# A graph layer on one Trainium2 core: the row that VectorE compares places with, in PSUM instead of SBUF

## The chip, the core and the metric

The kernel runs on one core of a Trainium2 chip. The metric is device time in microseconds: the median of the runs. PE is TensorE (matrix products), DVE is VectorE, ACT is ScalarE, POOL is GpSimd, SP is SyncE, which here only issues transfers. SBUF is the core's working memory with 128 partitions; PSUM is where products land, eight banks of 128 partitions by 512 fp32 numbers.

## The reference

One layer of a graph network with a gated update, over 12,500 nodes with 128 features and 400,000 edges with 32 features; the edges are sorted by their destination `dst`.

```python
h = jnp.maximum(_layernorm(x), 0.0)
e = jnp.concatenate([h[src], h[dst], edge_attr_32], axis=-1)
m = jax.nn.relu(e @ w1 + b1) @ w2 + b2
agg = jax.ops.segment_sum(m, dst, num_segments=12500)
gi, gh = agg @ w_ih + b_ih, h @ w_hh + b_hh
r, z = sigmoid(gi_r + gh_r), sigmoid(gi_z + gh_z)
n = tanh(gi_n + r * gh_n)
out = x + (1 - z) * n + z * h
```

## The kernel before, in words

**First stage (lines 207 to 334).** The nodes are normalised in chunks of four times 128. PE transposes each chunk into a PSUM tile named `oh` (line 296), DVE or ACT copies it to `hT_all` (line 315), a second product with the first 128 rows of `w1` lands in `pre` (line 325), and is copied and stored to DRAM as the table `A` (lines 305 and 320): `A` holds each node's contribution as a source. The tile `oh` comes from the pool `ps2`, which hands out two banks in turn.

**Edges (lines 842 to 935).** The edges are worked through in 391 pairs of up to 8 tiles of 128 edges; a pair is two units `u = 2k` and `2k + 1`. For each tile of most pairs, POOL issues a gather (line 145): an indirect transfer that reads 128 rows of `A` (for the first ten pairs, of `x`) by the indices in `src_i`, which lie in SBUF, into `G`. For 43 pairs nothing is gathered; there ACT (line 789, 19 pairs) or DVE (line 796, 24 pairs) copies the columns of `hT_all` one by one, at addresses loaded to registers, and PE multiplies them (line 612). Both are spread over the units from a list (`jobs`), not placed by a planner.

Since the edges are sorted, the destinations of a pair lie in two windows of 32 consecutive nodes. For each pair, DVE copies the windows' columns to `hw` (line 519), PE multiplies them with the second part of `w1` into an `oh` tile (line 526, the *product*), and DVE adds the bias on the way to `RW` (line 535). DVE builds a one-hot matrix of places as the left side of the next product (line 500), PE makes `pre` from it (line 601), DVE adds the gathered rows (line 626, the *add*), and ACT applies the relu (line 632).

To sum by destination, DVE builds a second one-hot matrix, `OH` (line 553, the *compare*): for each edge, the place of its destination in its window (`dloc`, fp16, in SBUF, one number for each partition and tile) is compared with the row 0..31 (`iota`, fp16, in SBUF, filled by POOL at line 117). Both operands are read with repeats, for 256 results in a partition, fp32. PE multiplies `OH` with the relu's output (line 645), and DVE and ACT take the sums out (lines 653 and 654).

**Nodes (lines 657 to 736).** After every 14 pairs the sums of a block of 512 nodes are placed, and the gates are computed in single steps (lines 699 to 734, among them DVE's lines 712, 715, 724, 726, 728 and 734), spread over the following units.

**Order.** The order on each engine is the one in which the program is written (`manual_schedule`); waits are put in where tiles depend on each other. In a pair, DVE makes the compare for pair k + 3 in the second unit, then the add, the bias step (535), and the window copy for pair k + 4 (519); PE makes the product for pair k + 3 in the first unit. POOL's queue holds little but the gathers in order; a gather waits only until its `G` buffer (7 in a ring, 4 more at the start) is free. One more user of an `oh` tile is `check_windows` (line 460), once, near the end. A branch for other inputs (line 1036 on) isn't taken here.

Of the kernel before, what the change touches and what calls it, by code (L numbers as in the profile page):

```python
# [8 lines left out]
F32 = mybir.dt.float32  # L9
# [10 lines left out]
N, E, D, DE = 12500, 400000, 128, 32  # L20
# [5 lines left out]
NP = T // PAIR + 1  # L26
NU = 2 * NP

V = 32
# [26 lines left out]
def tile_gnn(ctx: ExitStack, tc: tile.TileContext, x, src, srcT, dstT, dstP, eaT, eaP, w1, b1, w2T, b2,  # L56
             wih, bih, whh, bhh, out):
    nc = tc.nc
# [8 lines left out]
    ge = early.enter_context(tc.tile_pool(name="ge", bufs=EARLY, side="right"))  # L67
    ps2 = ctx.enter_context(tc.tile_pool(name="ps2", bufs=2, space=bass.MemoryType.PSUM))
    ps1 = ctx.enter_context(tc.tile_pool(name="ps1", bufs=1, space=bass.MemoryType.PSUM))
    dram = ctx.enter_context(tc.tile_pool(name="dram", bufs=1, space=bass.MemoryType.DRAM))  # L70

    def tiles(k):
        return (0 if k == 0 else SUP0 + (k - 1) * PAIR, SUP0 + k * PAIR)
# [11 lines left out]
    for m, n in SPREAD.items():  # L85
        lo, hi = {"dve": (JOBS0 + 3, NP - 9), "act": (JOBS0 + 11, NP - 6)}[m]
        for i in range(n):
            k = lo + int((i + 1) * (hi - lo) / n)
# [27 lines left out]
    iota = const.tile([128, V], F16, name="iota")  # L116
# [86 lines left out]
    def relu_norm(o, xi, st):  # L203
        nc.scalar.activation(o, xi, AF.Relu, bias=st[:, 1:2], scale=st[:, 0:1])
# [4 lines left out]
    with tc.tile_pool(name="pp", bufs=3) as pp:  # L209
# [6 lines left out]
        def nodes(t, i0, n, P):  # L216
            return t[i0 * 128:i0 * 128 + n * P, :].rearrange("(p i) f -> p i f", p=P)


        def columns(b, c, e):  # L220
            i0, n = bats[b]
            t = hT_all[:, i0 * 128:i0 * 128 + n * PB(b)].rearrange("f (p i) -> f i p", i=n)
            return t[:, c:e, :]

        def load(b):
            if b < len(bats):
                i0, n = bats[b]
                P = PB(b)
                xs[b] = pp.tile([128, 8, D], F32, name="xs", bufs=5)
                nc.sync.dma_start(xs[b][:P, :n, :], nodes(x, i0, n, P))  # L230
# [3 lines left out]
        def stat(b):  # L234
            if b < len(bats):
                i0, n = bats[b]
                mvs[b] = bn(pp, lambda j: xs[b][:PB(b), j, :], PB(b), n)

        def sqr(b):
            if b < len(bats):  # L240
                mvs[b] = bn_sqrt(pp, mvs[b], PB(b), bats[b][1])

        def fin(b):
            if b < len(bats):
                i0, n = bats[b]
                bn_fin(pp, st_all[:, i0:i0 + n, :], mvs.pop(b), PB(b), n)
# [32 lines left out]
        def chunk(q):  # L279
            b, c = chunks[q]  # L280
            i0, n = bats[b]
            return b, i0, c, min(n, c + 4), PB(b), (i0 + c) * 128

        pts, pas = {}, {}
        NC = len(chunks)
        for q in range(NC + 3):
            if q < NC:
                b, i0, c, e, P, n0 = chunk(q)
                if c == 0:
                    stat(b + 2)  # L290
                    fin(b + 1)
            if 1 <= q <= NC:
                b, i0, c, e, P, n0 = chunk(q - 1)
                pts[q - 1] = ps2.tile([128, 512], F32, name="oh")
                for j in range(c, e):
                    nc.tensor.transpose(pts[q - 1][:, (j - c) * P:(j - c + 1) * P],
                                        xs[b][:P, j, :], ident[:P, :P])
                if e == bats[b][1]:
                    load(b + 5)
            if q >= 3:  # L300
                b, i0, c, e, P, n0 = chunk(q - 3)
                if c == 0:
                    asb[b] = pp.tile([128, 8, D], F32, name="asb", bufs=2)
                copy = nc.scalar.copy if q % 4 == 2 else nc.vector.tensor_copy
                copy(asb[b][:P, c:e, :], pas.pop(q - 3)[:P, :e - c, :])
            if q < NC:
                b, i0, c, e, P, n0 = chunk(q)
                for j in range(c, e):
                    relu_norm(xs[b][:P, j, :], xs[b][:P, j, :], st_all[:P, i0 + j, :])
                if e == bats[b][1]:  # L310
                    sqr(b + 2)
            if 1 <= q <= NC:
                b, i0, c, e, P, n0 = chunk(q - 1)
                copy = nc.scalar.copy if q % 4 == 0 else nc.vector.tensor_copy
                copy(columns(b, c, e), pts.pop(q - 1)[:, :(e - c) * P].rearrange(
                    "f (i p) -> f i p", i=e - c))
            if q >= 3:
                b, i0, c, e, P, n0 = chunk(q - 3)
                if e == bats[b][1]:
                    nc.sync.dma_start(nodes(A, i0, e, P), asb[b][:P, :e, :])  # L320
            if 2 <= q <= NC + 1:
                b, i0, c, e, P, n0 = chunk(q - 2)
                pas[q - 2] = ps2.tile([128, GRP, D], F32, name="pre")
                for j in range(c, e):
                    nc.tensor.matmul(pas[q - 2][:P, j - c, :], columns(b, j, j + 1)[:, 0, :],
                                     w1a, start=True, stop=True)
        for b0, b1, n in ((0, 1, BAT[0]), (1, 12, 8), (12, 13, BAT[12])):
            i0 = sum(BAT[:b0])
            for b in range(b0, b1):
                i = i0 + (b - b0) * n  # L330
# [2 lines left out]
                    st_all[:, i:i + n, :].rearrange("p i o -> p (i o)"))  # L333
        nc.sync.dma_start(stats[NFULL * 128:N, :], st_all[:N - NFULL * 128, NFULL, :])

    p3 = ctx.enter_context(tc.tile_pool(name="p3", bufs=3, reuse_waits="tile"))
    TOT = p3.tile([128, 2 * BW - DMIN], F32, name="TOT", bufs=1)
    DEG = p3.tile([33, 2 * BW - DMIN], F32, name="DEG", bufs=1)
# [15 lines left out]
    pm = ps1.tile([128, 512], F32, name="misc")  # L354
# [65 lines left out]
    pm = ps1.tile([128, 512], F32, name="nd")  # L420
# [29 lines left out]
    def check_windows():  # L450
        m = const.tile([128, 2], F32, name="lim1")
        nc.vector.tensor_reduce(m[:, 0:1], lim[:, 0, :], AX.X, ALU.max)
        nc.vector.tensor_reduce(m[:, 1:2], lim[:, 1, :], AX.X, ALU.min)
        bad = const.tile([128, 2], F32, name="bad")
        nc.vector.tensor_scalar(bad[:, 0:1], m[:, 0:1], float(V - 1), None, op0=ALU.is_gt)
        nc.vector.tensor_scalar(bad[:, 1:2], m[:, 1:2], 0.0, None, op0=ALU.is_lt)
        one = const.tile([128, 1], F32, name="one")
        nc.vector.tensor_tensor(one, bad[:, 0:1], bad[:, 1:2], op=ALU.max)
        pm = ps2.tile([128, 512], F32, name="oh")
        nc.tensor.transpose(pm[0:1, :128], one, ident)  # L460
        f = const.tile([1, 8], F32, name="flags")
        nc.vector.tensor_reduce(f[:, 0:1], pm[0:1, :128], AX.X, ALU.max)
        nc.vector.tensor_reduce(f[:, 6:7], off_f, AX.XY, ALU.max)
        nc.vector.tensor_reduce(f[:, 7:8], off_f, AX.XY, ALU.min)
        nc.vector.tensor_scalar(f[:, 1:2], f[:, 6:7], float(BW - V - SHIFT), None, op0=ALU.is_gt)
        nc.vector.tensor_scalar(f[:, 5:6], f[:, 7:8], 0.0, None, op0=ALU.is_lt)
        nc.vector.tensor_reduce(f[:, 2:3], step_f, AX.X, ALU.max)
        nc.vector.tensor_scalar(f[:, 3:4], blk_f[:, NB - 1:NB], float(N - BW), None,
                                op0=ALU.not_equal)
        nc.vector.tensor_copy(f[:, 4:5], f[:, 5:6])  # L470
        nc.vector.tensor_reduce(f[:, 6:7], f[:, 0:6], AX.X, ALU.max)
        nc.vector.tensor_copy(flag, f[:, 6:7])
# [31 lines left out]
    bases, PB_, HW = {}, {}, {}  # L504
# [17 lines left out]
    def window_product(k):  # L522
        if k >= NP:
            return
        PB_[k] = ps2.tile([128, 512], F32, name="oh")
        nc.tensor.matmul(PB_[k][:2 * V, :D], HW.pop(k).rearrange("p a v -> p (a v)"), w1b,  # L526
                         start=True, stop=True)

# [8 lines left out]
    def onehot(k):  # L537
        if k >= NP:
            return
        t0, t1 = tiles(k)  # L540
        OH[k] = OHB[k % len(OHB)]
        for a in range(2) if k == 0 else (None,):
            if a is None:
                o, s = OH[k].rearrange("p j a v -> p a j v"), slice(t0, t1)
                d = dloc[:, s].rearrange("p (a j) -> p a j", a=2)[:, :, :, None]
                shape = [128, 2, GRP, V]
                i = iota[:, None, None, :]
            else:
                e = min(t1, (a + 1) * GRP)
                o, d = OH[k][:, :e - a * GRP, a, :], dloc[:, a * GRP:e, None]  # L550
                shape = [128, e - a * GRP, V]
                i = iota[:, None, :]
            nc.vector.tensor_tensor(o, d.to_broadcast(shape), i.to_broadcast(shape),  # L553
                                    op=ALU.is_equal)

# [294 lines left out]
    for k in range(3):  # L850
        window_copy(k)
        window_product(k)
        window_rows(k)
# [35 lines left out]
    for u in range(NU):  # L889
        k, h = divmod(u, 2)  # L890
# [145 lines left out]
    f = nc.values_load(flag[0:1, 0:1], min_val=0, max_val=1)  # L1036
# [67 lines left out]
```

## Time and profile before

| | |
|---|---|
| runs before | 3594.44, 3597.59, 3604.85 us; median 3597.59 |
| profiled execution | 3598.83 us, its span 3597.1 us |
| busy, share of the span | PE 74%, DVE 68%, ACT 70%, POOL 75% |
| mean granted clock of TensorE | 0.778 |
| DMA, mean over the span | 89 GB/s |

How to read the profile: a span is the time from the first to the last instruction of one profiled execution. A line of the table of groups gives source line, engine, operation, output and inputs with their shapes and the count, then the busy time in us with the mean of one in ns, then the idle time of the engine just before them and what ended it. "Issue" is time in which the engine waited for nothing that the profile shows: its own issuing, or loads of registers, which are not counted as busy. In the waits, a line says who waited for whom, for how many us in total, how often, and the longest. In the timeline, a line starts with start and duration in us.

### The profile page before, as it was taken

How to read it: one execution, taken by the hardware profiler on the slowest of the kernel's cores; microseconds unless marked ns; L12 is line 12 of the kernel's file. 1: busy time of each engine (PE TensorE's matmuls, PEld its weight loads, DVE VectorE, ACT ScalarE, POOL GpSimd, SP SyncE). 2: the span in 40 equal slices, each digit the busy share in tenths (PEclk: the TensorE clock that was granted, in tenths of full speed). 3: DMA queues.
4: the chain of work that ended last, by engine and by line, in shares of the span. 5: the costliest groups of instructions: out<-in, count | busy, mean ns of one | idle time of the engine just before them, and what ended most of it. 6: DMA issues, size and time to landing. Idle time of an engine off the chain costs nothing. (4 is left out here: it accounts for less than half of the span.)

```text
span 3597.1 us, 76803 instructions
## 1 busy us (share of the span) xinstructions
PE 2664.4 (74%) x13674; PEld 1618.5 (45%) x13674; DVE 2445.7 (68%) x16547; ACT 2506.7 (70%) x20936; POOL 2694.2 (75%) x2789
## 2 busy tenths in 40 slices
PE   7697677677767776876777777677767776776876
PEld 6454344444434443443444444444444443443443
DVE  8766667677667667667666677676667677766652
ACT  5445567777777777777777777777777677767771
POOL 7677777777777777777777777777777777777774
PEclk9787888787877877777786888787777778786777
DMA  6333333333333333333333333333333333333331
GB/s 207 86 100 87 86 88 88 92 86 89 87 88 85 87 89 85 89 86 89 86 86 89 86 88 88 92 87 88 88 87 86 85 89 84 89 85 87 81 86 41
DMA packets 145458, 321.60 MB, mean 89 GB/s; under 512 B 58913, under 2 KB 64844, under 8 KB 144967
## 3 DMA queue, kind: packets, MB, share of 16 engines
q0 software_dynamic: 88992, 182.43, 20.7%
q1 hardware_dynamic: 55831, 134.16, 13.5%
q14 instruction: 379, 3.10, 0.3%
q8 instruction: 112, 1.84, 0.2%
q10 hardware_dynamic: 144, 0.07, 0.0%
HBM read 302.60 MB, written 13.84 MB: 88 GB/s over the span
## 5 line engine op out<-in xcount | busy, mean ns | idle before, releaser
L145 POOL DMA_INDIRECT G<-A,src_i x2704 | 2620.3, 969 | 835.3 <-issue 780.1
L789 ACT COPY HE_act<-hT_all 128x4 uint8 x19456 | 1983.0, 189 | 585.6 <-issue 583.7
L796 DVE SCALAR_TENSOR_TENSOR both<-hT_all 128x4 uint16 x12288 | 1097.0, 155 | 954.0 <-issue 947.2
L601 PE MATMUL pre<-RW,L 128*128 128x256 f32 x3128 | 1171.0, 503 | 730.5 <-DVE G L626 633.8
L601 PEld LDWEIGHTS pre<-RW,L 128*128 128x128 f32 x3128 | 677.1, 241 | 1068.8 <-DVE G L626 811.0
L632 ACT ACTIVATE RB<-G 128x512 f32<-128x512 f32 x676 | 424.5, 628 | 353.5 <-issue 143.4
L645 PE MATMUL seg<-RB,OH 128*32 128x129 f32 x6250 | 642.8, 340 | 4.3 <-ACT dcol L654 4.3
L626 DVE TENSOR_TENSOR G<-pre,G 128x512 f32<-128x512 f32 x676 | 462.5, 684 | 64.1 <-DMA G<-A,src_i 41.7
L645 PEld LDWEIGHTS seg<-RB,OH 128*32 128x32 f32 x6250 | 349.5, 130 | 232.2 <-issue 127.9
L526 PE MATMUL oh<-w1b,hw 128*64 128x128 f32 x782 | 213.0, 364 | 123.8 <-DVE hw L519 120.4
L535 DVE TENSOR_TENSOR RW<-oh,b1b 32x128 f32<-32x128 f32 x782 | 217.2, 278 | 11.5 <-PE oh L526 6.2
L526 PEld LDWEIGHTS oh<-w1b,hw 128*64 128x64 f32 x782 | 91.6, 166 | 294.2 <-DVE hw L519 210.6
L500 DVE TENSOR_SCALAR L<-Ld,node_of 64x512 f32<-64x512 int32 x391 | 192.2, 492 | 0.7 <-issue 0.6
L553 DVE TENSOR_TENSOR OH<-dloc,iota 128x256 f32<-128x256 f16 (+1 forms) x392 | 161.0, 411 | 0.2
L676 PE MATMUL nd<-spot,sums 64*128 64x40 f32 x782 | 116.9, 319 | 0.0
L676 PEld LDWEIGHTS nd<-spot,sums 64*128 64x128 f32 x782 | 113.0, 229 | 7.9 <-issue 7.9
L653 DVE COPY sums<-seg 64x128 f32<-64x128 f32 x391 | 107.1, 274 | 4.9 <-PE seg L645 3.7
L640 PE MATMUL seg<-zrow 1*64 1x129 bf16 x391 | 106.4, 272 | 3.0 <-ACT dcol L654 3.0
L519 DVE COPY hw<-hT_all 128x64 f32 x391 | 87.6, 224 | 24.6 <-issue 23.4
L801 DVE COPY HE_dve<-both 128x512 uint8<-128x512 uint8 x192 | 88.0, 458 | 6.6
L145 POOL DMA_INDIRECT G<-in_x,src_i x77 | 73.0, 948 | 25.1 <-issue 22.9
L640 PEld LDWEIGHTS <-zrow 1*64 1x64 bf16 x391 | 43.4, 111 | 94.7 <-issue 94.7
(148 smaller groups left out, 1605.0 us busy)
## 6 DMA issues: line engine op xcount, KB each, us to landing
Ld<-in_dstP SPq DMA_DIRECT2D x390, 128.0 KB
L<-in_eaP SPq DMA_DIRECT2D x195, 256.0 KB
G<-A,src_i POOLq DMA_INDIRECT x2704
xb<-in_x SPq DMA_DIRECT2D x28, 256.0 KB
out<-xb SPq DMA_DIRECT2D x28, 256.0 KB
xs<-in_x SPq DMA_DIRECT2D x11, 512.0 KB
A<-asb SPq DMA_DIRECT2D x11, 512.0 KB
src_i<-in_srcT SPq DMA_DIRECT2D x19, 80.0 KB
```

Source lines behind the costliest of these rows:

```text
L145: nc.gpsimd.indirect_dma_start(out=G[k][:, j, a, :], out_offset=None, in_=table, in_offset=bass.IndirectOffsetOnAxis(ap=src_i[c][:, i:i + ...
L500: nc.vector.tensor_scalar(Ls[k // QP][:2 * V, c], Ds[k // QP][:, c], node_of[:, k:k + 1], None, op0=ALU.is_equal)
L526: nc.tensor.matmul(PB_[k][:2 * V, :D], HW.pop(k).rearrange("p a v -> p (a v)"), w1b, start=True, stop=True)
L535: nc.vector.tensor_tensor(RW[k % 4][s, a, :], pm[s, :D], b1b[s, :], op=ALU.add)
L553: nc.vector.tensor_tensor(o, d.to_broadcast(shape), i.to_broadcast(shape), op=ALU.is_equal)
L601: nc.tensor.matmul(PP[u][:, 2 * i:2 * i + 2, :], Ls[k // QP][:, c0:c0 + 128], RW[k % 4], start=True, stop=not raw)
L626: nc.vector.tensor_tensor(RT[u], PP.pop(u), RT[u], op=ALU.add)
L632: nc.scalar.activation(o[:, :, :D], RT.pop(u), AF.Relu)
L645: nc.tensor.matmul(SEG[k][V * a:V * (a + 1), :D + 1], OH[k][:, j, a, :], RB[u % 3][:, (j % 2) * 2 + a, :D + 1], start=False, stop=all(b != ...
L676: nc.tensor.matmul(pt[:, bass.ds(offs[i], V + SHIFT)], sums[:, i, :], spot, start=False, stop=i == n - 1)
L789: nc.scalar.copy(he[:, e * 4:e * 4 + 4], column(v))
L796: nc.vector.scalar_tensor_tensor(both[:, (e0 % PIECE + i) // 2, :], column(vals[i + 1]), 256.0, column(vals[i]), op0=ALU.mult, op1=ALU.add)
```

## The change

Two PSUM tiles `wide` of 128 x 512 are allocated once and for all, in place of the two rotating `oh` tiles of pool `ps2`; the number of banks in use stays the same. The first stage's transposes, the products and `check_windows` use them in turn. After the first stage, DVE copies `iota` (fp16) into columns 128 to 159 of both (fp32 there). A product writes columns 0 to 127 of the bank `k % 2`; the compare for pair k reads the row from the other bank, `(k + 1) % 2`. The compare's first operand `dloc` and its output stay in SBUF.

```diff
+    wide = [ps1.tile([128, 512], F32, name=f"wide{i}") for i in range(2)]
...
-                pts[q - 1] = ps2.tile([128, 512], F32, name="oh")
+                pts[q - 1] = wide[q % 2]
...
+    for w in wide:
+        nc.vector.tensor_copy(w[:, D:D + V], iota)
     p3 = ctx.enter_context(tc.tile_pool(name="p3", bufs=3, reuse_waits="tile"))
...
-        pm = ps2.tile([128, 512], F32, name="oh")
+        pm = wide[(NP - 20) % 2]
         nc.tensor.transpose(pm[0:1, :128], one, ident)
...
-        PB_[k] = ps2.tile([128, 512], F32, name="oh")
+        PB_[k] = wide[k % 2]
         nc.tensor.matmul(PB_[k][:2 * V, :D], HW.pop(k).rearrange("p a v -> p (a v)"), w1b,
...
         OH[k] = OHB[k % len(OHB)]
+        row = wide[(k + 1) % 2][:, D:D + V]
...
-                i = iota[:, None, None, :]
+                i = row[:, None, None, :]
...
-                i = iota[:, None, :]
+                i = row[:, None, :]
             nc.vector.tensor_tensor(o, d.to_broadcast(shape), i.to_broadcast(shape),
                                     op=ALU.is_equal)
```

## The prediction

> **What bounds the kernel now.** I read four views in this order: the table of costliest groups, the waits, the chain that ended last, and the timeline. The groups:
>
> ```profile
> L145 POOL DMA_INDIRECT G<-A,src_i x2704 | 2620.3, 969 | 835.3 <-issue 780.1
> L626 DVE TENSOR_TENSOR G<-pre,G 128x512 f32<-128x512 f32 x676 | 462.5, 684 | 64.1 <-DMA G<-A,src_i 41.7
> L553 DVE TENSOR_TENSOR OH<-dloc,iota 128x256 f32<-128x256 f16 (+1 forms) x392 | 161.0, 411 | 0.2
> L145 POOL DMA_INDIRECT G<-in_x,src_i x77 | 73.0, 948 | 25.1 <-issue 22.9
> ```
>
> POOL issues 2704 + 77 = 2781 gathers. Their busy time is 2620.3 + 73.0 = 2693.3 us and the gaps ahead of them 835.3 + 25.1 = 860.4 us: 3553.7 us together, and the last gather ends at 3553.9 of a span of 3597.1. So POOL does nothing but gathers, back to back. The waits say why the gaps are there:
>
> ```profile
> POOL G L145 <- issue: 803.0, 2635, 0.3
> POOL G L145 <- PE misc L586: 11.6, 1, 11.6
> DVE G L626 <- DMA G<-A,src_i: 41.7, 20, 4.3
> DVE node_of L365 <- POOL place_c L360: 13.1, 1, 13.1
> ```
>
> Each line gives microseconds, times and the longest. The gap is a fixed 0.3 us of issue; POOL waits for a buffer only once (11.6 us, in the start). The others wait for POOL: the add of line 626 sat 41.7 us until gathers landed. The chain that ended last shows the same at its start: gather, issue, gather, then a tail of 43 us without gathers.
>
> ```profile
> 3551.59 0.30 issue
> 3551.90 0.95 POOL G L145
> 3552.84 0.30 issue
> 3553.15 0.77 POOL G L145
> ```
>
> So every nanosecond that a gather gets shorter moves the end, as long as the consumers keep up. The commonest gather lasts 0.944 us (the median of the view of line 145; its minimum is 0.940, its maximum 2.132). 2693.3 - 2781 x 0.944 = 68.0 us are excess. The timeline shows where excess comes from (start, duration):
>
> ```profile
> 1110.20 0.42 DVE L553 TENSOR_TENSOR OH<-dloc,iota 128x256 f32<-128x256 f16 x1
> 1110.20 1.23 POOL L145 DMA_INDIRECT G<-A,src_i  x1 [0.30 <-issue]
> ```
>
> ```profile
> 420.33 0.69 DVE L626 TENSOR_TENSOR G<-pre,G 128x512 f32<-128x512 f32 x1
> 420.75 0.94 POOL L145 DMA_INDIRECT G<-A,src_i  x1 [0.30 <-issue]
> ```
>
> ```profile
> 1198.65 0.41 DVE L553 TENSOR_TENSOR OH<-dloc,iota 128x256 f32<-128x256 f16 x1
> 1198.66 1.22 POOL L145 DMA_INDIRECT G<-A,src_i  x1 [0.30 <-issue]
> ```
>
> A gather that starts with a compare of line 553 takes 1.22 to 1.23 us; one that starts inside the add of line 626, with 0.27 us of it left, takes 0.94. The compare has both inputs in SBUF, the add has one in PSUM. Over the whole trace, gather by gather: the excess is (end of the compare) - (start of the gather) - 0.124 us, with a spread of 0.004. So 0.124 us after its start a gather needs something that the compare holds to its end. 117 gathers fit this for line 553 within 25 ns, with **26.1 us** of excess. Against it: 153 gathers reach that point in the middle of an add of line 626 and have a mean excess of -0.1 ns and a largest of 3 ns. Lines 712, 715 and 734, with the SBUF input first and the other in PSUM as in the changed compare, give 21 more, none over 3 ns. The steps at 724, 726 and 728, same shape but both inputs in SBUF, do stall gathers (29 of them, 10.5 us).
>
> The 26.1 follows from rows too: a gather starts every 3553.7 / 2781 = 1.278 us, a compare holds 0.412 us, so by chance 391 x 0.412 x 0.412 / (2 x 1.278) = 26.0 us.
>
> **The change part by part.**
>
> *The compare's second input moves to PSUM (391 pairs).* By the rows above the compare then has its operands where lines 712, 715 and 734 have theirs, and stalls no gather: -26.1 us. Not all is won: 31 of the 117 gathers began over 0.06 us ahead of the compare, and most of those were held first by the step before it, nearly always line 796, which also has two SBUF inputs and hands over to the compare. Held to that step's end alone they would keep 3.6 us. Net **-22.5 us** on POOL. The other blockers stay (line 500 11.6 us, line 801 5.9, line 796 3.8, the gate steps).
>
> [...]
>
> *The compare's own duration.* At 512 elements the rows with one PSUM input last 668 to 687 ns (lines 626, 712, 715, 734) and those with two SBUF inputs 672 to 683 (724, 726, 728); at 128 elements 278 (line 535) against 283 (line 553, first pair). So -15 to +15 ns on 411: -6 to +6 us of DVE over 391 compares. A farther row is the plain copy of 128 elements: 274 ns from PSUM (line 653), 203 from SBUF (line 436), 71 ns more. I take 0, by the rows of the same operation, and keep 71 ns for the range. DVE isn't the last to end: the 41.7 us at line 626 is its cover. In the trace the time from a pair's gather to its add shrinks from 36 us at 500 to 23 at 2000; first at 2400 does the add wait for the gather (1.7 us behind). So the consumers are a little faster than POOL and have about 41.7 us in hand; the gain uses 22.5 and leaves 19.2. 33.0 of the 41.7 lie after 3200, mostly in the last pairs, where the hand-made columns are over and only POOL is late.
>
> [...]
>
> *Two copies of the row to PSUM*, 128x32. Nearest rows: 181 ns (line 553 at 32 elements) and 274 (line 653). About 0.4 us on DVE, ahead of the 13.1 us in which line 365 waits for POOL: nothing. Uncovered it is 0.4 us.
>
> *Fixed banks for the rotating pair* (lines 296, 460, 526). In the built order, the steady part has the same instructions with the same waits on every engine; the product still waits for hw and alternates over two banks, and the bank that a compare reads gets its next product only after the window copy that DVE makes behind that compare. In the first stage some matmuls lose a wait on PE, and one ScalarE copy gains one on DVE; behind it stand the later ScalarE copies and the loads of `xs`. POOL issues raw gathers until 98.6 us without waiting for that stage, and DVE idles 13.1 us before line 365: a shift of some us is hidden there; beyond 13 it would count fully. I take 0. The tail of 43 us has no compare: 0.
>
> *Sum:* the profiled execution took 3598.83 us (span 3597.1), so 3598.83 - 22.5 = 3576.3. The median of before is 1.2 lower: **3575.1**. With the stalls fully gone (26.1, and 2 more for luck in where the other blockers fall) 3569; with a fifth fewer (18) 3580.
>
> **The rivals.**
>
> 1. *The consumers become the bound.* If each compare gets longer by more than 19.2 / 391 = 49 ns (DVE alone setting their pace), DVE eats the rest of its slack. With the copies' 71 ns, 27.8 us: 3597.6 - 41.7 + 27.8 = 3583.7; with 80 ns 3587. For it: the copies at lines 653 and 436. Against: two-input rows are equal with and without PSUM.
>    [...]
> 2. *No gain*: the compare still holds what the gather needs, because a broadcast SBUF input beside PSUM behaves otherwise than lines 712 and 715. Then 3597.6, give or take 3. For it: every PSUM row has dense inputs. Against: 153 + 21 gathers without a stall.
> 3. *Slower: reading the 32 columns eight times from PSUM with repeats runs at a lower rate.* The nearest bad row is line 315, a copy from PSUM with a scattered output: 1078 ns against 685 for the plain one (line 588), 0.77 ns for each element more. For 256 elements that is 0.197 us, 77 us over 391: 3597.6 - 41.7 + 77 = 3633. It costs time from 41.7 / 391 = 107 ns per compare on. Against: the repeat is on the reading side, and the dense runs are 32 long.
>
> **How the numbers follow.** Forecast 0.75 (3569 to 3580, and about 3 us of run spread; before ran 3594.4 to 3604.9); rival 1 0.11; rival 2 0.08; rival 3 0.06. The range takes forecast and rival 1: 3566 to 3587. A change under 0.3% (11 us) can't be told from none here. Faster by more: the forecast and nearly all of rival 1, 0.85; same 0.09; slower 0.06.
>
> **What would show it.** Gathers: mean of line 145 from 969 to about 961 ns, POOL busy from 2694 to about 2672 us, issue unchanged at 0.30 each; no gather lengthened beside a compare. The compare: 396 to 426 ns. Line 626 waiting for gathers: from 41.7 to about 19 us. Wrong would be: compares over 460 ns, gathers of 1.2 us beside compares, or POOL idle on a buffer in the steady part.

## The result and the profile after

The changed kernel takes 3569.06 us (median of six runs, 3566.62 to 3576.31), the kernel before 3602.15 (six runs, 3594.44 to 3605.86): ratio 0.9915, 95% interval 0.9904 to 0.9926, about 31 us less. On the chips of eight of the experiments every version, the kernel before too, took 4837 to 4970 us instead of about 3600; POOL is not last there, so their times can't be set beside the others.

The groups of the changed kernel (line, engine, operation, count, busy us, mean ns of one, idle before; lines are 1 to 4 higher than before):

```profile
L146 POOL DMA_INDIRECT G<-A,src_i x2704 | 2595.4, 960 | 835.2 <-issue 780.4
L630 DVE TENSOR_TENSOR G<-pre,G 128x512 f32<-128x512 f32 x676 | 463.2, 685 | 37.1 <-PE pre L605 16.6
L557 DVE TENSOR_TENSOR OH<-dloc,wide 128x256 f32<-128x256 f16 (+1 forms) x392 | 159.8, 408 | 0.1
L146 POOL DMA_INDIRECT G<-in_x,src_i x77 | 72.8, 946 | 25.1 <-issue 22.9
```

The gathers' busy time fell from 2693.3 to 2595.4 + 72.8 = 2668.2 us; their gaps are the same. The compare takes 408 ns where it took 411. Above 0.944 us for each gather, 68.0 us of excess became 43.0: **25.0 us less on POOL**. The waits of the changed kernel (us, times, longest):

```profile
POOL G L146 <- issue: 803.2, 2636, 0.3
...
POOL G L146 <- PE misc L590: 11.6, 1, 11.6
...
DVE G L630 <- DMA G<-A,src_i: 10.9, 3, 4.3
```

POOL still waits for nothing but its own issue and the one buffer at the start; the gaps that the view puts down to other engines are of the same 0.3 us each. The add (line 630) waits 10.9 us for gathers, 41.7 before. And the timeline beside a compare of the changed kernel:

```profile
1729.37 0.42 DVE L557 TENSOR_TENSOR OH<-dloc,wide 128x256 f32<-128x256 f16 x1
1729.38 0.94 POOL L146 DMA_INDIRECT G<-A,src_i  x1 [0.30 <-issue]
```

The gather starts with the compare, as at 1110.20 and 1198.66 in the kernel before, and takes 0.94 us, not 1.22.

Where did the rest go? The last gather ended at 3555.3 us of the span before and ends at 3530.2 now: 25.2 us, POOL's part. The end behind it went from 41.7 to 34.7 us, another 7.0. Its products, before and after (start, duration, from the two chains that ended last):

```profile
3574.00 2.00 PE misc L695 x2
3576.00 2.00 PE misc L697 x2
3578.01 2.00 PE nd L695 x2
```

```profile
3548.74 1.12 PE misc L699 x2
3549.86 1.06 PE misc L701 x2
3550.91 1.05 PE nd L699 x2
```

The same pairs of products take 2.0 us in one and 1.05 in the other. Before, all ten such pairs of the tail took 1.7 to 2.0 us; after, the first three did, and the other seven took 0.9 to 1.1. The granted clock of TensorE was 0.50 from 3560 us to the end before, and 0.67 over the last 30 us after. The change doesn't touch these products.

### The profile page after: what moved, and what is told of

It reads as the page before. It is cut to its first block, busy times and chain, and to the rows that moved or that the text cites. A ratio compares the mean times of both kernels' runs of the same rounds, so it can differ in the third digit from the quotient of the medians.

```text
span 3564.8 us, 76807 instructions
## 1 busy us (share of the span) xinstructions
PE 2651.2 (74%) x13674; PEld 1617.2 (45%) x13674; DVE 2443.6 (69%) x16549; ACT 2505.0 (70%) x20936; POOL 2669.2 (75%) x2789
## 5 line engine op out<-in xcount | busy, mean ns | idle before, releaser
L146 POOL DMA_INDIRECT G<-A,src_i x2704 | 2595.4, 960 | 835.2 <-issue 780.4
L649 PE MATMUL seg<-RB,OH 128*32 128x129 f32 x6250 | 635.6, 337 | 3.7 <-ACT dcol L658 3.7
L529 PE MATMUL wide<-w1b,hw 128*64 128x128 f32 x782 | 208.8, 357 | 121.5 <-DVE hw L522 115.6
L538 DVE TENSOR_TENSOR RW<-wide,b1b 32x128 f32<-32x128 f32 x782 | 216.9, 277 | 12.4 <-PE wide L529 7.1
L529 PEld LDWEIGHTS wide<-w1b,hw 128*64 128x64 f32 x782 | 90.0, 163 | 292.4 <-DVE hw L522 208.9
L557 DVE TENSOR_TENSOR OH<-dloc,wide 128x256 f32<-128x256 f16 (+1 forms) x392 | 159.8, 408 | 0.1
L680 PEld LDWEIGHTS nd<-spot,sums 64*128 64x128 f32 x782 | 121.9, 245 | 8.9 <-issue 8.9
L680 PE MATMUL nd<-spot,sums 64*128 64x40 f32 x782 | 125.7, 334 | 0.0
L146 POOL DMA_INDIRECT G<-in_x,src_i x77 | 72.8, 946 | 25.1 <-issue 22.9
```

The lines of the kernel that those rows point to most:

```text
L146: nc.gpsimd.indirect_dma_start(out=G[k][:, j, a, :], out_offset=None, in_=table, in_offset=bass.IndirectOffsetOnAxis(ap=src_i[c][:, i:i + ...
L538: nc.vector.tensor_tensor(RW[k % 4][s, a, :], pm[s, :D], b1b[s, :], op=ALU.add)
L649: nc.tensor.matmul(SEG[k][V * a:V * (a + 1), :D + 1], OH[k][:, j, a, :], RB[u % 3][:, (j % 2) * 2 + a, :D + 1], start=False, stop=all(b != ...
L680: nc.tensor.matmul(pt[:, bass.ds(offs[i], V + SHIFT)], sums[:, i, :], spot, start=False, stop=i == n - 1)
```

## The experiments

Twelve experiments were run; e0 and h0 are the changed kernel itself, f1 repeats e1, and f3 and h3 repeat e3. Stalls are counted as in the prediction: gathers whose excess ends with one kind of step, 0.820 us ahead of the gather's end, within 25 ns. "Gate steps" are the three with both inputs in SBUF.

| run | median us | kernel before, same chip | ratio (95%) | held by the compare | by the gate steps |
|---|---|---|---|---|---|
| before | 3602.15 | | | 26.1 us, 117 gathers | 10.5 us |
| after | 3569.06 | 3602.15 | 0.9915 (0.9904 to 0.9926) | 0.0 us, 1 | 10.7 us |
| e0 | 4863.72 | 4869.35 | 0.9988 (0.9968 to 1.0007) | 0, 0 | 6.7 |
| e1 | 4864.66 | 4869.35 | 0.9998 (0.9976 to 1.0020) | 16.7, 85 | 5.8 |
| e2 | 4867.97 | 4869.35 | 0.9993 (0.9968 to 1.0017) | 12.7, 46 | 7.0 |
| e3 | 4862.39 | 4869.35 | 0.9979 (0.9960 to 0.9998) | 0, 0 | 0 |
| f1 | 4860.23 | 4870.81 | 0.9989 (0.9968 to 1.0011) | 18.1, 94 | 6.3 |
| f3 | 4934.53 | 4936.50 | 0.9995 (0.9981 to 1.0008) | 0.0, 1 | 0 |
| g1 | 3991.14 | 3591.11 | 1.1108 (1.1090 to 1.1127) | 44.0, 172 | 5.5 |
| g2 | 3951.33 | 3591.11 | 1.0999 (1.0981 to 1.1017) | 0, 0 | 11.9 |
| g3 | 3939.79 | 3591.11 | 1.0963 (1.0947 to 1.0979) | 0, 0 | 0 |
| g4 | 3987.63 | 3591.11 | 1.1099 (1.1081 to 1.1116) | 44.7, 170 | 3.8 |
| h0 | 4948.05 | 4951.72 | 0.9995 (0.9976 to 1.0015) | 0, 0 | 7.3 |
| h3 | 4949.39 | 4951.72 | 0.9996 (0.9979 to 1.0012) | 0, 0 | 0.2 |

### e0 to e3: the change again, its parts, and one step further

e0 is the changed kernel.

> The changed kernel once more, for a second profile of its end. Theory (the compare no longer holds what a gather needs): POOL busy 2669 us again, within 4, and the last gather ends about 25 us sooner than in the profile before (3555.3). The end after the last gather was 41.8 us before and 34.6 after. If that difference is only the granted clock (products of 512 columns in pairs of 2.0 us against 1.05), it scatters between 34 and 42 from profile to profile of any kernel. Rival (the change itself shortens the end): 34 to 36 us here and in each kernel with the row in PSUM, 41 to 42 in those without.

e1:

```diff
+    row_s = const.tile([128, V], F32, name="row_s")
+    nc.vector.tensor_copy(row_s, iota)
...
-        row = wide[(k + 1) % 2][:, D:D + V]
+        row = row_s
```

> The changed kernel with its two fixed banks and its copies, but the compare reads the row from an fp32 copy in SBUF. Theory (two SBUF inputs hold the gathers): all of the gain is gone, ratio to before 1.000 (0.997 to 1.003), POOL busy about 2694 us, gathers of about 1.2 us beside compares again. Rivals: the fixed banks or the shorter waits make the gain: ratio 0.991 as in the changed kernel; the fp32 row instead of the fp16 one makes it: the same 0.991.

e2:

```diff
-        row = wide[(k + 1) % 2][:, D:D + V]
+        row = wide[(k + 1) % 2][:, D:D + V] if k % 2 else iota
```

> The changed kernel, with the row read from PSUM for odd pairs and from SBUF for even pairs. Theory: each compare is worth the same, so half of the 25 us on POOL, 12 to 13 us: POOL busy about 2681 us, ratio to before 0.9955 (0.993 to 0.998). Rival (few bad phases make most of the gain, or it comes from elsewhere): all of it or none.

e3:

```diff
-        nc.scalar.activation(t, t, AF.Tanh)
-        z = temp()
-        nc.scalar.activation(z, pz, AF.Sigmoid)
+        nc.scalar.activation(pi, t, AF.Tanh)
+        t, z = pi, pz
+        nc.scalar.activation(z, pz, AF.Sigmoid)
```

> The changed kernel, and the gate steps too get one PSUM input: tanh and the second sigmoid write into the banks of their inputs, so the three steps of VectorE that had both inputs in SBUF read one from PSUM. Theory: their stalls (10.7 us in the profile after, 34 gathers) go as well; POOL busy about 2658 us. The consumers have only about 11 us in hand (the add waited 10.9 us for gathers in the profile after), so at most about 11 us of it reach the end: ratio to before 0.988 to 0.990 (against 0.9915). Rival (the hold is peculiar to repeated inputs of the compare): no change against the changed kernel, 0.9915.

The ratios of e2 and e3 did not come out as expected. That of e1 did, 0.9998, but it says nothing, since e0, with the change in full, came to 0.9988. POOL's busy time, expected at 2669, 2694, 2681 and 2658 us, came out at 2657, 2671, 2677 and 2646. POOL's waits in e0 say why the times don't move:

```profile
POOL G L146 <- ACT RB L636: 1172.3, 288, 18.4
POOL G L146 <- issue: 779.1, 2331, 24.8
```

POOL waited 1172.3 us for the relu to free its buffers; a gather that is done sooner only waits longer. In the same profile ScalarE's column copies waited 1587.5 us for issue, where they waited 583.7 in the profile of the kernel before. Why issue was so much slower on these chips stays open. So the times of e0 to e3 say little about the theory, except for one thing: where the consumers are last, no gain from the change is shown (e0: 0.9988, with an interval of 0.9968 to 1.0007, so 0.3% at most). Only the interval of e3 lies just below 1.

The stalls of the four do answer. With the row in PSUM no gather is held by the compare (e0, e3). With the row in SBUF, fp32 and beside the fixed banks (e1), 85 are. With every other compare on PSUM (e2) 46 are, and all 46 by the half that reads `iota`:

```profile
L557 DVE TENSOR_TENSOR OH<-dloc,iota 128x256 f32<-128x256 f16 x195 | 80.6, 413 | 1.8 <-issue 1.8
L557 DVE TENSOR_TENSOR OH<-dloc,wide 128x256 f32<-128x256 f16 x195 | 79.9, 410 | 2.6 <-issue 2.5
```

Same kernel, same count, nearly the same busy time; the place of one operand differs (and its type, fp16 in SBUF and fp32 in PSUM; e1 has fp32 in SBUF and holds gathers). In e3 the gate steps hold no gather either, so it is not peculiar to the compare's repeated inputs.

### f1 and f3: the same on other chips

f1 is the kernel of e1, f3 that of e3.

> The kernel of e1 again (fixed banks and copies kept, row read from an fp32 copy in SBUF), since in the runs of e0 to e3 both kernels took 1.36 times as long and POOL waited for buffers. Where before takes about 3600 us: theory (two SBUF inputs hold the gathers): ratio to before 1.000 (0.997 to 1.003), POOL busy about 2694 us. Rivals (fixed banks, or the fp32 row): ratio 0.991, POOL busy about 2669 us. Where before takes about 4870 us again, neither shows in the time.

> The kernel of e3 again, for its time where before takes about 3600 us. Theory: POOL busy about 2658 us (2669 in the changed kernel), no gather held by the three gate steps, and since the add waited only 10.9 us for gathers in the profile after, the consumers are about to become the last: ratio to before 0.988 to 0.990 (the changed kernel: 0.9915, 0.9904 to 0.9926). Rival (nothing left to win, the consumers are already the last): 0.9915. Where before takes about 4870 us again, POOL waits over 1100 us for buffers and the ratio is 0.997 to 1.000 for every version.

Both met chips of the longer time again; their stalls repeat those of e1 and e3.

### g1 to g4: POOL made last on purpose

To read times at all, the four give POOL more to do and the consumers less:

```diff
-SPREAD = {"dve": 24, "act": 19}
+SPREAD = {"dve": 1, "act": 1}
```

g1 is the kernel before with this, g2 the changed one, g3 that of e3, g4 that of e1.

> The kernel before with two pairs instead of 43 whose columns are copied by hand: 3109 gathers instead of 2781, and hardly any column copies on VectorE and ScalarE. It computes the same. It is the base of the next three, meant to make POOL the last again where the consumers were. If POOL sets the pace: 3109 x 1.249 us plus about 55 us of stalls, 12 us of the one buffer wait and 45 us of start and end, about 3995 us, with about 26 us of stalls by the compare (391 x 0.412 x 0.412 / (2 x 1.27)). If the consumers still set it: above 4100 us, and POOL waits for buffers.

> The changed kernel with the same two pairs copied by hand, against g1 on the same chip. Theory (the compare with one PSUM input holds no gather, and POOL is last): no stall by the compare and 23 to 28 us less than g1, 0.6 to 0.7 per cent. Rival (the gain is a matter of the consumers or of the banks): less than 5 us.

> As g2, with the three gate steps reading one input from PSUM. Theory: the consumers have far more in hand here, so the stalls of the gate steps (about 10 us) go into the time in full: 8 to 12 us less than g2. Rival (a step that reads PSUM costs its gain elsewhere): equal to g2.

> As g2 (fixed banks, their copies), but the row is read from an fp32 copy in SBUF. Theory: the time of g1 within 4 us, stalls by the compare about 26 us. Rivals (fixed banks or the fp32 row make the gain): the time of g2.

g1 came out at 3991.14 us, 3995 expected, and POOL sets the pace. Its waits, and below them its gathers and those of g2:

```profile
POOL G L145 <- issue: 923.9, 3032, 0.3
POOL G L145 <- PE misc L586: 11.6, 1, 11.6
```

```profile
DVE G L626 <- DMA G<-A,src_i: 2186.8, 670, 5.8
```

```profile
L145 POOL DMA_INDIRECT G<-A,src_i x3032 | 2917.8, 962 | 935.2 <-issue 901.0
```

```profile
L146 POOL DMA_INDIRECT G<-A,src_i x3032 | 2881.3, 950 | 935.1 <-issue 895.2
```

670 of the 758 adds of g1 wait for their gather (676 adds in the kernel before, with fewer gathers). g2 is 39.8 us faster than g1 (medians on the same chip; 37.5 between the two profiled executions); its gathers of `A` alone are busy 36.5 us less. g4, with the banks and the copies but the row in SBUF, is 3.5 us from g1: the rivals that the fixed banks, the shorter waits or the fp32 row make the gain fall here. g3 takes another 11.5 us off g2, with the 11.9 us of stalls by the gate steps gone: a second change of the same kind paid in full here, where POOL is last.

The direction was as expected, the size of g2 not: 23 to 28 us were expected. The compare of g1 held gathers for 44.0 us, not 26. The difference lies in gathers that were already waiting when the compare began. In g1 there are 33 of them with 18.7 us, 22 behind the last gate step (line 728); the other 139 have 25.3 us, which is near the estimate by chance (26). Such a hand-over in the timelines of g1 and g2:

```profile
1779.65 0.67 DVE L728 TENSOR_TENSOR gt<-gt 128x512 f32<-128x512 f32 x1
...
1779.93 1.55 POOL L145 DMA_INDIRECT G<-A,src_i  x1 [0.30 <-issue]
...
1780.25 0.41 DVE L553 TENSOR_TENSOR OH<-dloc,iota 128x256 f32<-128x256 f16 x1
```

```profile
1763.09 0.68 DVE L732 TENSOR_TENSOR gt<-gt 128x512 f32<-128x512 f32 x1
1763.39 1.20 POOL L146 DMA_INDIRECT G<-A,src_i  x1 [0.30 <-issue]
1763.69 0.41 DVE L557 TENSOR_TENSOR OH<-dloc,wide 128x256 f32<-128x256 f16 x1
```

In g1 the gather is held to the end of the compare (1780.66 - 1779.93 - 0.124 = 0.61 us over 0.944), though the gate step ended 0.34 us sooner. In g2 it is held to the end of the gate step (1763.77 - 1763.39 - 0.124 = 0.26) and goes on while the compare runs. So the part that belongs to the step ahead stays (the steps at line 732 hold 6.6 us in g2, those at 728 none in g1 by this count), and 44.0 us of stalls give 36.6 on POOL.

### h0 and h3: the changed kernel and e3 once more

h0 is the changed kernel, h3 that of e3.

> The changed kernel once more, for its ratio and a second profile of its end where before takes about 3600 us. Theory: the last gather ends about 25 us before the 3555.3 of the profile before, and the 7 us by which the end behind it was shorter (34.7 against 41.7 us) was the granted clock: the four kernels g1 to g4 had 33.6 to 34.6 us with and without the change. So the ratio to before is 0.992 to 0.994 if before's usual end is as short as these, and 0.991 if it is usually about 41 us. Where before takes about 4870 us again, nothing of this can be read.

> The kernel of e3 once more. Theory: no gather held by the gate steps; the consumers had 10.9 us in hand in the profile after, so up to that much of the 10.7 us reaches the end: ratio to before 0.988 to 0.991, 2 to 11 us less than h0. Rival (the consumers are already the last): equal to h0 within 2 us.

Again chips of the longer time. Of the end, g1 to g4 tell what h0 was to tell: 34.3, 33.6, 34.6 and 34.5 us behind the last gather, with the row in SBUF and in PSUM alike. In g1 and g2 the last seven pairs of products took 0.9 to 1.3 us, and in g2 the granted clock was 0.67 over the last 30 us. So the change does not shorten the end; the profile before had a slower clock there, 0.50. e3 has not been timed where POOL is last with all 43 pairs copied by hand, so whether it beats the changed kernel there stays open.

## Why the prediction was right

- **POOL is last, back to back.** Right. The gathers' gaps are 0.3 us of issue in both kernels, and the last gather ends 25.2 us sooner for 25.0 us less excess. One reading was careless: 3553.9 is where the shown piece of the chain stops, not the end of the last gather. That one starts at 3554.4 and ends at 3555.3, so the tail is 41.7 us, not 43. No step hangs on it.
- **A compare with one PSUM input holds no gather.** Right: 26.1 us became 0.0. e1, e2 and g4, with 16.7, 12.7 and 44.7 us held, show that it is this operand, not the banks, the waits or fp32.
- **The step ahead takes part of it back (3.6 us).** Right in kind and size: the stalls that end with the hand copies rose from 3.8 to 7.2 us. Net 22.5 us were forecast, 25.0 measured on POOL: 26.1 - 3.4 = 22.7 from these two, and 2.3 more from gathers held by other steps. The range had 2 us for such luck, the sum nothing.
- **The estimate by chance, 26.0 us.** It met 26.1 partly by luck. Only 17.3 us of that are compares that came upon a gather about to read; 8.8 are hand-overs, 17 gathers. g1 shows that the two parts are separate: 25.3 and 18.7.
- **The compare's own time.** 408 ns, forecast 396 to 426. The 71 ns between the two plain copies, kept for the range, are not there: in e2 the half with the row in SBUF takes 413 ns, the half with it in PSUM 410.
- **The consumers keep up.** Right, but with less to spare: 10.9 us of waiting left at the add, 19 forecast. Of the 8 between, 2.5 are POOL's larger gain; what took the rest isn't shown. The reading that the consumers are a little faster than POOL does not hold throughout: in the profile after, the add starts 23 us behind its last gather at 870 us and 42 behind at 2140, where before it stayed at 22 to 24; only then does it catch up, to 26 at 3400. Rival 1, consumers last because the compare gets longer, did not happen. On the chips where issue was slower the consumers were last without it, and no gain was shown (e0: 0.9988).
- **Rivals 2 and 3.** No gain: refuted by the stalls (26.1 us before, 0.0 after). Slower by reading in repeats: refuted by the 408 ns.
- **The size in time.** 3575.1 forecast, 3569.06 measured. The sum had 22.5 us; by the ratio the change gave about 31 (27 to 35), of which POOL's part is 25. So the mechanism is right and its sum falls short: that the time lies so far down in the range is in part luck. In the one profile pair the rest is the clock in the tail (7.0 us; 0.50 before, 0.67 after), a term that the sum had at 0 and that g1 to g4 show to be none of the change's doing. Whether that is so in most runs, or whether the run spread makes up the rest, was not settled.

In the kernel before, 117 gathers were held by a `tensor_tensor`, the compare, with 26.1 us; what in a gather it is that waits, no run here shows.

## What to carry to other kernels

Where POOL issues indirect gathers back to back and is last, look for the VectorE steps with two SBUF inputs beside them, and put one input in PSUM if a bank is there: here the compare took 408 ns where it had taken 411, and the stalls that end with it fell from 26.1 us to 0.0. They are not the only steps to look for. In the kernel before, line 500 compares one tensor in SBUF with one number for each partition, line 801 copies one tensor from SBUF to SBUF, and both hold gathers to their end by the same sum:

```profile
463.22 0.47 DVE L500 TENSOR_SCALAR L<-Ld,node_of 64x512 f32<-64x512 int32 x1
463.38 1.13 POOL L145 DMA_INDIRECT G<-A,src_i  x1 [0.30 <-issue]
```

The gather takes 0.19 us over 0.944, and 463.69 - 463.38 - 0.124 = 0.19. All 112 gathers of that profile that reach the point of 0.124 us at least 0.22 us after such a step began are held to its end, 72 by line 500 and 40 by line 801; of the 78 that reach it in the first 0.15 us, none is. Together the two lines hold 17.5 us, and the change leaves that as it is (17.4 after). No experiment moved their operands, so what they share with the compare isn't shown.

Count the stalls by where each one ends, not by averages, and ask who holds the gather next when one holder is gone. Before that, see who waits for whom: the same edit gave 0.9% where POOL was last and no gain that could be told from none where POOL waited for buffers.

## What the runs showed of the hardware

- The hold passed from one VectorE step with two SBUF inputs to the next without letting the gather in: a gather of 2.13 us in the kernel before (at 2754.84 us) started with a gate step (line 728) and was held to the end of the compare behind it, with four steps of line 796 in between, 1.19 us over 0.944.
- The hold was exact: excess = end of the step - start of the gather - 0.124 us, with a standard deviation of 4 ns over the 117 gathers of the compare in the kernel before.
- The tail, which the change doesn't touch, took 33.6 to 41.7 us from profile to profile where POOL was last, with pairs of products of 512 columns at 1.05 us or 2.0 us; the granted clock was 0.67 in the short tails of the changed kernel and of g2, and 0.50 in the long one.
- Chips differed far more than this change: for the kernel before 3591 us on the chip of g1 to g4 and 3602 in the runs of the result, 4869 to 4952 on four others. Each of the four was met in one set of runs, so whether it is the chip or the time of the run isn't shown.
